# A four-layer conditioned sequence model on one core: which TensorE tilings stand next to each other in attention, MLP and experts

## Chip, core and metric

The kernel runs on one core of a Trainium2 chip. The metric is the device time of one execution in microseconds (us); less is better. The core has five engines that run side by side and wait for each other by semaphores: TensorE (PE, its weight loads are shown apart as PEld), VectorE (DVE), ScalarE (ACT), GpSimd (POOL) and SyncE (SP, which here issues DMAs).

## The reference, cut to what matters

The input is `x` of 4 sequences x 512 tokens x 288 channels in fp32 and a condition of 4 x 288. Four layers follow each other:

```python
x = x + (z @ expm(A(cond)) - z) @ U.T            # L0: z = x @ U, U from a QR of P
# L1 and L2: transformer blocks, modulated by cond; 16 heads of 18 channels
h = layernorm(x) * (1 + scale) + shift
q, k, v = split(h @ W_qkv + b_qkv)               # L2 also normalizes q and k per head
x = x + gate * (softmax(q @ k.T * 18**-0.5) @ v) @ W_proj
x = x + gate2 * gelu(modulate(layernorm(x)) @ w1 + b1) @ w2      # 288 -> 1152 -> 288
# L3: the same attention, then 4 experts, each token through its best 2
moe = sum_e cw[:, e] * (gelu(xn @ w1[e] + b1[e]) @ w2[e] + b2[e])
out = x + gate2 * moe
```

## The kernel before, in words

**Tilings.** TensorE can be used as one array of 128 rows x 128 columns or as smaller arrays side by side. A matmul's operands choose it: a contraction over 32 rows uses a 32x128 tiling (four such matmuls can run at once, on four row groups), an output of 32 partitions uses a 128x32 tiling (four at once, on four column groups). Every product of this kernel is in fp32, and the trace shows each matmul as two passes (a transpose as one).

**Channels.** The 288 channels are held as two slices of 128 (`KW = 2`) and a tail of 32, and the tail is repeated on three strips of 32 partitions (`strip(i)`). A product over channels is thus two dense matmuls (128x128 tiling) and one tail matmul (32x128 tiling), and the tails of up to three products can run side by side on three row groups.

**Blocks.** One attention block `n` (0 to 11) is one layer and one sequence; blocks 0 to 3 are layer L1, 4 to 7 L2, 8 to 11 L3. `attend(n, ...)` walks through 4 groups `G` of 4 heads, each in 8 steps `s`, so 32 steps a block. In each step

- `maxima` computes scores of two heads, 10 steps ahead (`p_s`, two matmuls of 32x128 tiling), and VectorE reduces them to row maxima (TENSOR_REDUCE `store<-p_s`);
- `weigh` computes the transposed scores of two other heads (`p_st`, two matmuls of 32x128 tiling, on the other two row groups, so beside `p_s`), and ScalarE takes the exponential (`e<-p_st`);
- in step `s = 6`, `take_maxima(G + 1)` transposes the maxima of the next group (`p_m`), and VectorE subtracts them from that group's queries (`store<-store,p_m`); `weigh` of the next group reads those queries from its step 0 on;
- in even steps `give_values` multiplies one key tile `c` (two steps' exponentials) with the values (`sum_values`, `p_av`, four matmuls of 128x32 tiling side by side); after the fourth key tile the sums are copied out (`o`);
- then other work fills TensorE: the generators in `fill`, each of which yields a cost after each piece. `left` grows by `total / 32` a step, 0.5 more in odd and 0.5 less in even steps, and pieces are taken while it is positive. The pieces are the next block's layernorm transposes (`p_t`) and projections (`project`: `p_qk`, `p_v`, in L2 also `p_var`), the last block's output projection (`finish`: `p_o`), and in blocks 10 and 11 the routing of tokens to experts (`route`, `place`). `norms` brings one piece of VectorE's layernorm work a step.

`project` goes through its products in pairs: the dense matmuls of both, then the two tails in one piece, then their evictions by ScalarE or VectorE. `p_s` and `p_st` share one PSUM ring of two buffers (`pbig`), so that each waits until the last one of its kind has been read. `pmm` is a PSUM ring of three buffers, used by nearly everything else; `pacc` is one buffer, for `p_av`.

**MLP.** After each of the blocks 1 to 8 the MLP of block `n - 1` runs alone (`mlp`, `hidden`, `mlp_out`): three groups of three hidden slices, each 12 dense passes (`p_h`), then the three tails side by side, then three Gelus; after the first group `between()` gives one key tile of values. Then `p_y`.

**Experts.** At the end 19 tiles of 256 tokens go through the experts (`tile_pieces`): again three groups of three slices (`p_he`: dense, tails, Gelus on ScalarE to `hide`), with a `yield` after each; then the transposes of the next tile (`p_te`, `p_tf`) and the second product (`p_ye`, 36 passes). At each yield a piece of the remaining routing (`others`) runs, six a tile, in tiles 0 to 3. POOL gathers a tile's weights and tokens and scatters its sums by indirect DMA.

**Order.** From the first column of L0 on, TensorE, ScalarE and VectorE keep the order in which the program text issues their instructions (`keep_in_program_order`), so the loops above are the order on the engines, and each engine runs its own list from the front.

Of the kernel before, what the change touches and what calls it, by code (L numbers as in the profile page):

```python
# [9 lines left out]
F32 = mybir.dt.float32  # L10
# [7 lines left out]
NT = 4  # L18
# [5 lines left out]
NG = 4  # L24
# [23 lines left out]
def cond_seq_kernel(ctx: ExitStack, tc: tile.TileContext, a: dict, out: bass.AP):  # L48
# [230 lines left out]
    md = mods.tile([128, C], F32, name="md")  # L279
# [17 lines left out]
    def modulations(ns):  # L297

        for n in ns:
# [4 lines left out]
            gr = mods.tile([B, C], F32, tag="gr", name=f"gr{n}")  # L304
# [11 lines left out]
            if half and l < 2:  # L316
                br = mods.tile([B, C], F32, tag="br", name=f"br{l}")
# [3 lines left out]
            if n == 5:  # L321
                sr = mods.tile([B, C], F32, tag="br", name="sr")
# [38 lines left out]
    with tc.tile_pool(name="l0", bufs=1) as l0, tc.tile_pool(name="l0w", bufs=2) as l0w, \  # L361
# [7 lines left out]
        At = mods.tile([D, C], F32, name="At")  # L369
# [327 lines left out]
    def hidden(pool, tag, bufs, l, b, h, w1, b1, func, between=lambda: None):  # L697

        gs = []
        for f0 in range(0, NF, 3):  # L700
            p = pbig(f"p_h{l}_{b}_{f0}")
            p = [p[:, 0, :], p[:, 1, :], pmm(f"p_h{l}_{b}_{f0 + 2}")]
            cols = [slice((f0 + i) * 128, (f0 + i + 1) * 128) for i in range(3)]
            for i in range(3):
                for k in range(KW):
                    matmul(p[i], w1[:, k, cols[i]], h[:, k, :], start=(k == 0), stop=False)
            for i in range(3):
                matmul(p[i], w1[strip(i), KW, cols[i]], h[strip(i), KW, :], start=False, stop=True)
# [6 lines left out]
            if f0 == 0:  # L715
                between()
        return gs
# [293 lines left out]
    with tc.tile_pool(name="attn", bufs=2) as at:  # L1011
# [15 lines left out]
        def project(n, norm):  # L1027

            l, b = divmod(n, B)
# [6 lines left out]
            def qk_job(m):  # L1036
# [4 lines left out]
                def evict():  # L1041
# [4 lines left out]
                    else:  # L1046
                        tmp = at.tile([128, 2, T], F32, tag="e", name=f"tmp{n}_{m}", bufs=6)
                        sq, rs = tmp[0:w, 0, :], tmp[0:w, 1, :]
# [24 lines left out]
            for i in range(0, len(jobs), 2):  # L1073
# [7 lines left out]
                for e in later:  # L1081
                    yield from e
                for q, (p, operands, evict) in enumerate(pair):
# [106 lines left out]
        def attend(n, fill, total, norms):  # L1190

            left = 0.0
            for step in range(8 * NG):
# [8 lines left out]
                if s == 8 - 2 and G + 1 < NG * NB:  # L1202
                    take_maxima(G + 1)
                if s % 2 == 0:
                    give_values()
                left += total / (8 * NG) + (0.5 if s % 2 else -0.5)
                next(norms, None)
                while left > 0:
                    cost = next(fill, "end")
                    if cost == "end":  # L1210
                        break
                    left -= cost or 0.0
# [7 lines left out]
        def give_values():  # L1220

            if not ready:
                return
            G, c = ready.pop()
# [289 lines left out]
```

## Time and profile before

| | |
|---|---|
| median of 3 runs | 2094.88 us (2086.53 to 2099.71) |
| the profiled execution | 2086.44 us |
| its span, first to last instruction | 2084.7 us |
| busy: PE / DVE / ACT / POOL | 91% / 45% / 37% / 12% |
| mean granted TensorE clock | 0.957 |
| attention blocks 0 to 11, with the MLPs between | 213.7 to 1647.5 us |
| experts | 1655.8 us to the end |
| scores' maxima on VectorE (384) | 470.4 us, 1225 ns each |
| exponentials on ScalarE (384) | 393.1 us, 1024 ns each |

A row of the profile names line, engine and operation, what is written and read (`out<-in`, buffer numbers left out), the shape, how many, and after a bar the busy time and mean duration and the idle time of the engine just before, with what ended it. In the timeline a row is a start, a time from first start to last end, and a merged group of like instructions; `[0.32 <-DVE store L60]` is idle time before it and what ended it. The page's busy time is an average over stages: a busy TensorE is not the same as a TensorE that sets the pace.

### The profile page before, as it was taken

To read this page: it belongs to the slowest core of one execution; us is meant where nothing else is said; L and a number is where in the kernel's file an instruction comes from. 1 tells how busy PE (TensorE), PEld (TensorE's weight loads), DVE (VectorE), ACT (ScalarE), POOL (GpSimd) and SP (SyncE) were. 2 spreads that over 40 slices of the span, in tenths; PEclk is the share of its full clock that TensorE was granted. 3 is DMA by queue.
4 is the path that set the end of the run, shared out by engine and by line. 5 is a ranking of instruction groups with operands and counts; after the bars stand their busy time and mean duration, and the time that the engine had idled before them with its cause. 6 is when DMAs were issued, how large, how long until landed. Compare 5 with 4: busy or idle time off the path is not lost. (4 is left out here: it accounts for less than half of the span.)

```text
span 2084.7 us, 26249 instructions
## 1 busy us (share of the span) xinstructions
PE 1901.0 (91%) x10269; PEld 927.7 (44%) x10269; DVE 928.8 (45%) x1953; ACT 781.3 (37%) x1169; POOL 252.2 (12%) x362
## 2 busy tenths in 40 slices
PE   6769879999999999899999999998987899999997
PEld 4544223343523434234234343333322367777775
DVE  6764646346164362562634526355576334111111
ACT  5122454434254343443444434444444322212111
POOL 1000010001010020010100000000000212332322
PEclk9578999999999999999999999999999989999999
DMA  3212152031131221511203112061221445766663
GB/s 97 71 40 62 37 153 81 17 96 29 40 73 26 72 58 42 135 42 54 75 22 85 33 54 80 23 137 30 82 50 61 172 147 175 238 187 219 203 202 95
DMA packets 89420, 187.23 MB, mean 90 GB/s; under 512 B 25454, under 2 KB 50457, under 8 KB 86803
## 3 DMA queue, kind: packets, MB, share of 16 engines
q1 hardware_dynamic: 77462, 103.39, 18.8%
q0 software_dynamic: 11248, 79.79, 11.8%
q10 hardware_dynamic: 584, 2.36, 0.4%
q8 instruction: 81, 1.33, 0.3%
q14 instruction: 45, 0.36, 0.1%
HBM read 152.49 MB, written 55.45 MB: 100 GB/s over the span
## 5 line engine op out<-in xcount | busy, mean ns | idle before, releaser
L60 DVE TENSOR_REDUCE store<-p_s 128x2 f32<-128x1024 f32 x384 | 470.4, 1225 | 370.3 <-PE p_st L60 324.0
L60 ACT ACTIVATE e<-p_st 128x1024 f32<-128x1024 f32 x384 | 393.1, 1024 | 643.9 <-PE p_st L60 639.6
L60 PE MATMUL p_s<-store 32*128 32x512 f32 x1536 | 445.4, 652 | 83.0 <-DVE store L60 81.7
L60 PE MATMUL p_st<-store 32*128 32x512 f32 x1536 | 444.2, 655 | 0.9 <-DVE store L60 0.9
L60 PEld LDWEIGHTS p_s<-store 32*128 32x128 f32 x1536 | 120.6, 186 | 315.9 <-DVE store L60 230.1
L60 PE MATMUL p_av<-e,store 128*32 128x512 f32 x1536 | 212.5, 626 | 2.0 <-ACT e L60 2.0
L60 PE MATMUL p_he<-hTe,store 128*128 128x256 f32 (+1 forms) x1026 | 200.1, 404 | 4.2 <-DVE hTe L60 4.2
L60 PE MATMUL p_ye<-store,hide 128*128 128x288 f32 x684 | 175.0, 415 | 7.2 <-ACT hide L60 7.2
L60 ACT ACTIVATE hide<-p_he,store 128x256 f32<-128x256 f32 x171 | 68.7, 472 | 281.7 <-PE p_he L60 281.7
L60 PEld LDWEIGHTS p_he<-hTe,store 128*128 128x128 f32 (+1 forms) x1026 | 147.7, 191 | 53.0 <-issue 30.5
L695 POOL TENSOR_TENSOR x<-x,gated 128x288 f32<-128x288 f32 x80 | 64.0, 800 | 837.0 <-DVE gated L60 837.0
L60 PE MATMUL p_qk<-hT,wqk 128*126 128x512 f32 (+1 forms) x360 | 162.3, 619 | 0.3 <-DVE store L60 0.3
L60 PE MATMUL p_h<-hT,w 128*128 128x512 f32 (+1 forms) x432 | 156.7, 618 | 5.2 <-DVE store L60 5.2
L60 PEld LDWEIGHTS p_ye<-store,hide 128*128 128x128 f32 x684 | 130.3, 193 | 46.9 <-ACT hide L60 11.0
L60 DVE TENSOR_TENSOR gated<-p_y,gate 128x288 f32<-128x288 f32 x32 | 14.7, 458 | 286.2 <-PE p_y L60 286.2
L60 PE MATMUL p_y<-w,hid 128*128 128x288 f32 x576 | 141.8, 407 | 0.0
L60 PEld LDWEIGHTS p_y<-w,hid 128*128 128x128 f32 x576 | 108.8, 190 | 35.5 <-issue 6.1
L60 PEld LDWEIGHTS p_st<-store 32*128 32x128 f32 x1536 | 118.0, 186 | 9.2 <-issue 6.2
L60 PEld LDWEIGHTS p_h<-hT,w 128*128 128x128 f32 (+1 forms) x432 | 60.7, 189 | 99.7 <-issue 83.6
L60 PE MATMUL p_o<-wp,oc 126*128 126x288 f32 (+1 forms) x288 | 94.6, 450 | 1.3 <-DVE oc L60 1.3
L60 DVE COPY hTe<-p_te 128x512 f32<-128x512 f32 x19 | 13.1, 690 | 172.9 <-PE p_tf L60 127.8
L60 PEld LDWEIGHTS p_qk<-hT,wqk 128*126 128x126 f32 (+1 forms) x360 | 46.9, 177 | 95.9 <-issue 94.3
(248 smaller groups left out, 1723.1 us busy)
## 6 DMA issues: line engine op xcount, KB each, us to landing
store<-qd SPq DMA_DIRECT2D x96, 144.0 KB
qd<-stage SPq DMA_DIRECT2D x48, 252.0 KB
od<-o SPq DMA_DIRECT2D x192, 36.0 KB
rd<-rd SPq DMA_DIRECT2D x12, 576.0 KB
oc<-od SPq DMA_DIRECT2D x24, 252.0 KB
rb<-rd SPq DMA_DIRECT2D x24, 252.0 KB
etab<-in_L_cond_w_dram SPq DMA_DIRECT2D x4, 1296.0 KB
etab<-in_L_cond_w_dram SPq DMA_DIRECT2D x8, 576.0 KB
```

The lines of the kernel that those rows point to most:

```text
L60: ins = f(*args, **kw)
L695: nc.gpsimd.tensor_add(x[b][:, j, :], x[b][:, j, :], t)
```

## The change

- **Values.** `give_values` gives all key tiles that are ready, oldest first, and `attend` calls it at steps 0 and 4 alone: two key tiles (8 matmuls of 128x32 tiling) in one run instead of one in each even step. These two steps take no fill piece; the other six take pieces, `left` growing by `total / 24` in each.
- **Projections' tails.** `project` yields `"strips"` ahead of a pair's tails. `attend` then stops taking pieces, and takes the tails first thing after the next step's scores.
- **Maxima.** `take_maxima` moves from `s = 6` to `s = 7`, behind that step's tails and `norms` piece and ahead of its fill pieces.
- **MLP.** The tails of the second group of three slices run at once after those of the first, as the first matmuls of their sums, and its dense passes follow later; `between()` now gives two key tiles.
- **Experts.** All nine tails of a tile run in one go: six slices' dense passes first (two slices to a PSUM bank), then nine tails, then six Gelus are issued, then the last three slices' dense passes and their Gelus. There are still six yields in a tile: after two slices, after four, after all nine, and then as before.
- **Buffers.** Small tiles (`md`, `gr`, `br`, `At`) become parts of one tile `spare`, and L2's squares and reciprocal deviations in `project` lie in it too, so that they no longer take buffers of the ring `e`. In block 2 `give_values` is called once more after the steps.

```diff
--- before.py
+++ after.py
@@ -276,7 +276,9 @@
-    md = mods.tile([128, C], F32, name="md")
+
+    spare = mods.tile([128, 4 * C], F32, name="spare")
+    md = spare[:, 0:C]
...
-            gr = mods.tile([B, C], F32, tag="gr", name=f"gr{n}")
+            gr = spare[0:B, C:2 * C]
...
-                br = mods.tile([B, C], F32, tag="br", name=f"br{l}")
+                br = spare[0:B, 2 * C:3 * C]
...
-                sr = mods.tile([B, C], F32, tag="br", name="sr")
+                sr = spare[0:B, 2 * C:3 * C]
...
-        At = mods.tile([D, C], F32, name="At")
+        At = spare[0:D, 3 * C:]
...
@@ -696,16 +698,32 @@
 
     def hidden(pool, tag, bufs, l, b, h, w1, b1, func, between=lambda: None):
 
+
         gs = []
+
+        def banks(f0):
+            p = pbig(f"p_h{l}_{b}_{f0}")
+            return [p[:, 0, :], p[:, 1, :], pmm(f"p_h{l}_{b}_{f0 + 2}")]
+
+        def cols(f):
+            return slice(f * 128, (f + 1) * 128)
+
+        def tails(p, f0, first):
+            for i in range(3):
+                matmul(p[i], w1[strip(i), KW, cols(f0 + i)], h[strip(i), KW, :], start=first, stop=not first)
+
         for f0 in range(0, NF, 3):
-            p = pbig(f"p_h{l}_{b}_{f0}")
-            p = [p[:, 0, :], p[:, 1, :], pmm(f"p_h{l}_{b}_{f0 + 2}")]
-            cols = [slice((f0 + i) * 128, (f0 + i + 1) * 128) for i in range(3)]
+            if f0 != 3:
+                p = banks(f0)
             for i in range(3):
                 for k in range(KW):
-                    matmul(p[i], w1[:, k, cols[i]], h[:, k, :], start=(k == 0), stop=False)
-            for i in range(3):
-                matmul(p[i], w1[strip(i), KW, cols[i]], h[strip(i), KW, :], start=False, stop=True)
+                    matmul(p[i], w1[:, k, cols(f0 + i)], h[:, k, :], start=(k == 0 and f0 != 3),
+                           stop=(k == KW - 1 and f0 == 3))
+            if f0 != 3:
+                tails(p, f0, False)
+            if f0 == 0:
+                ahead = banks(3)
+                tails(ahead, 3, True)
             for i in range(3):
                 f = f0 + i
                 if f % 2 == 0:
@@ -714,6 +732,7 @@
                 gs.append(t[:, f % 2, :])
             if f0 == 0:
                 between()
+                p = ahead
         return gs
 
     def mlp_out(l, b, j, gs, w2):
@@ -1026,6 +1045,7 @@
 
         def project(n, norm):
 
+
             l, b = divmod(n, B)
             wqk, wv = WA[l][:2]
             h = hT[0]
@@ -1044,8 +1064,7 @@
                     if l != 1:
                         scalar.activation(t, p[0:w], AF.Identity, bias=bias, scale=scol[0:w, m:m + 1])
                     else:
-                        tmp = at.tile([128, 2, T], F32, tag="e", name=f"tmp{n}_{m}", bufs=6)
-                        sq, rs = tmp[0:w, 0, :], tmp[0:w, 1, :]
+                        sq = rs = spare[0:w, m % 2 * T:(m % 2 + 1) * T]
                         scalar.activation(sq, p[0:w], AF.Square, bias=bias)
                         vector.tensor_scalar(t, p[0:w], bias, None, ALU.add)
                         yield 0.0
@@ -1080,6 +1099,7 @@
                     pair.append((p, operands, evict))
                 for e in later:
                     yield from e
+                yield "strips"
                 for q, (p, operands, evict) in enumerate(pair):
                     matmul(p, *operands(KW, strip(q)), start=False, stop=True)
 
@@ -1189,7 +1209,7 @@
 
         def attend(n, fill, total, norms):
 
-            left = 0.0
+            left, strips = 0.0, False
             for step in range(8 * NG):
                 g, s = divmod(step, 8)
                 G = NG * n + g
@@ -1199,17 +1219,22 @@
                         next(fill)
                     maxima(ahead, mstep)
                 E.append(weigh(G, s))
-                if s == 8 - 2 and G + 1 < NG * NB:
-                    take_maxima(G + 1)
-                if s % 2 == 0:
+                if strips:
+                    left -= next(fill)
+                    strips = False
+                next(norms, None)
+                if s % 4 == 0 and ready:
                     give_values()
-                left += total / (8 * NG) + (0.5 if s % 2 else -0.5)
-                next(norms, None)
-                while left > 0:
-                    cost = next(fill, "end")
-                    if cost == "end":
-                        break
-                    left -= cost or 0.0
+                else:
+                    left += total / (6 * NG)
+                    if s == 8 - 1 and G + 1 < NG * NB:
+                        take_maxima(G + 1)
+                    while left > 0:
+                        cost = next(fill, "end")
+                        strips = cost == "strips"
+                        if cost == "end" or strips:
+                            break
+                        left -= cost or 0.0
                 if s % 2:
                     ready.append((G, s // 2))
             for _ in fill:
@@ -1219,14 +1244,14 @@
 
         def give_values():
 
-            if not ready:
-                return
-            G, c = ready.pop()
-            if c == 0:
-                PO[0] = pacc(f"p_av{G}")
-            sum_values(G, PO[0], c, E[:2])
-            del E[:2]
-            if c == NT - 1:
+            while ready:
+                G, c = ready.pop(0)
+                if c == 0:
+                    PO[0] = pacc(f"p_av{G}")
+                sum_values(G, PO[0], c, E[:2])
+                del E[:2]
+                if c < NT - 1:
+                    continue
                 t = at.tile([128, T], F32, tag="o", name=f"o{G}", bufs=3)
                 scalar.copy(t, PO[0])
                 n, g = divmod(G, NG)
@@ -1296,7 +1321,8 @@
             if t == 8:
                 take_maxima(0)
             next(rest, None)
-            next(new)
+            if next(new) == "strips":
+                next(new)
             if t == 5:
                 projection_bias(0)
         for n in range(NB):
@@ -1352,6 +1378,8 @@
             if 2 <= n < 2 + 2 * NE:
                 fill_table(n - 2)
             attend(n, itertools.chain(*fill), total, first_ready(side))
+            if n == 2:
+                give_values()
             if n == 2 or n == B + 2:
                 projection_bias(l + 1)
                 head_biases(l + 1)
@@ -1422,19 +1450,45 @@
             w1, w2, b1, b2 = expert_tile(store[t % 2])
             h = HT.pop(t)
             g = pool2.tile([128, NF, TS], F32, tag="hid", name=f"hide{t}")
-            for f0 in range(0, NF, 3):
-                p = pbig(f"p_he{t}_{f0}")
-                p = [p[:, 0, :TS], p[:, 1, :TS], pmm(f"p_he{t}_{f0 + 2}")[:, :TS]]
-                cols = [slice((f0 + i) * 128, (f0 + i + 1) * 128) for i in range(3)]
-                for i in range(3):
-                    for k in range(KW):
-                        matmul(p[i], w1[:, k, cols[i]], h[:, k, :], start=(k == 0), stop=False)
-                for i in range(3):
-                    matmul(p[i], w1[strip(i), KW, cols[i]], h[strip(i), KW, :], start=False, stop=True)
-                for i in range(3):
-                    f = f0 + i
-                    scalar.activation(g[:, f], p[i], AF.Gelu_apprx_tanh, bias=b1[:, f:f + 1])
-                yield
+
+
+
+            def dense(f, first, last):
+                for k in range(KW):
+                    matmul(p[f], w1[:, k, f * 128:(f + 1) * 128], h[:, k, :], start=(first and k == 0),
+                           stop=(last and k == KW - 1))
+
+            def tails(fs, first):
+                for f in fs:
+                    matmul(p[f], w1[strip(f % 3), KW, f * 128:(f + 1) * 128], h[strip(f % 3), KW, :],
+                           start=first, stop=3 <= f < 6)
+
+            def gelus(fs):
+                for f in fs:
+                    scalar.activation(g[:, f], p[f], AF.Gelu_apprx_tanh, bias=b1[:, f:f + 1])
+
+            p = {}
+            for f0 in (0, 6):
+                q = pbig(f"p_he{t}_{f0}")
+                if f0 == 0:
+                    for n in range(2):
+                        for f in (3 * n, 3 * n + 1):
+                            p[f] = q[:, f % 3, n * TS:(n + 1) * TS]
+                            dense(f, n == 0, False)
+                        yield
+                    q = pmm(f"p_he{t}_2")
+                    for f in (2, 5):
+                        p[f] = q[:, f // 3 * TS:(f // 3 + 1) * TS]
+                        dense(f, f == 2, False)
+                    tails(range(6), False)
+                else:
+                    p[6], p[7], p[8] = q[:, 0, :TS], q[:, 1, :TS], pmm(f"p_he{t}_8")[:, :TS]
+                    tails(range(6, NF), True)
+                    gelus(range(6))
+                    for f in range(6, NF):
+                        dense(f, False, True)
+                    gelus(range(6, NF))
+            yield
             if t + 1 < TILES:
                 tokens_T(t + 1)
                 if t + 2 < TILES and t + 2 != EARLY:
```

## The prediction

> **What bounds the kernel now.** I read the page first, then the groups, the waits, and the timeline of one step. The page makes it TensorE, and the groups name its largest stops.
>
> ```profile
> PE 1901.0 (91%) x10269; PEld 927.7 (44%) x10269; DVE 928.8 (45%) x1953; ACT 781.3 (37%) x1169; POOL 252.2 (12%) x362
> ...
> L60 DVE TENSOR_REDUCE store<-p_s 128x2 f32<-128x1024 f32 x384 | 470.4, 1225 | 370.3 <-PE p_st L60 324.0
> ...
> L60 PE MATMUL p_s<-store 32*128 32x512 f32 x1536 | 445.4, 652 | 83.0 <-DVE store L60 81.7
> ```
>
> VectorE's maxima take 1225 ns each, and TensorE stood 81.7 us before scores, waiting for VectorE. The timeline of block 8 shows how:
>
> ```profile
> 1250.89 0.70 PE L60 MATMUL p_s<-store 32*128 32x512 f32 x2
> ...
> 1251.96 1.07 PE L60 MATMUL p_av<-e,store 128*32 128x512 f32 x8
> 1252.06 1.23 DVE L60 TENSOR_REDUCE store<-p_s 128x2 f32<-128x1024 f32 x1 [1.27 <-PE p_st L60]
> ...
> 1253.34 0.70 PE L60 MATMUL p_s<-store 32*128 32x512 f32 x2 [0.32 <-DVE store L60]
> ```
>
> Scores take 1.07 us (1250.89 to 1251.96); their maxima are done 1.33 later; the next scores start 2.45 after the last. So a step lasts at least **2.46 us**, or as long as TensorE's own work in it if that is more. Of 372 steps (31 in each block, the last one runs into the MLP) 110 last 2.44 to 2.48.
>
> **What a change of tiling costs.** Start-to-start times give it. Four dense passes of 512 columns between scores take 1.92 (708.70 to 710.62); the first MLP group after 1073.37 takes 6.41 to the values at 1079.78, for 12 dense passes and 2 slots of tails. 4a + b = 1.92 and 14a + 2b = 6.41 give a = 0.43 a pass and b = 0.20 a run, whatever its length. A run of one key tile's values takes 0.99 (1079.78 to 1080.77), so b = 0.14 there; its second pass starts 0.45 after the first (1.07 for the group less 0.62, the mean of one), so two key tiles in one run take 3 x 0.45 + 0.54 = 1.90 where two runs take 1.99. Other passes: 0.24 at 288 columns, 0.22 at 256, 0.11 for a transpose, b = 0.09 for a run of them.
>
> The built order has 1237 changes of tiling before and 956 after. Pricing each run so, TensorE's own work falls by 36 us in attention, rises by 1.5 in the MLPs (moved values) and falls by 13.6 in the experts: **48 us** in all.
>
> [...]
>
> **Attention steps.** For each of the 372 steps I added TensorE's work from its scores to the next scores in both built orders and took 2.46 where that is less. In block 8 before: 80.0 us of work, 13 steps below the floor and short of it by 7.1, sum 87.2; the trace has 87.2 (1240.0 to 1327.2). The first eight of block 8, in us of TensorE's work: 1.60 (scores 0.96 + 4 transposes), 3.21, 2.07 (scores 1.07 + one key tile 0.99), 2.98 (scores + four dense passes 1.92), 2.07, 3.09, 2.49, 2.98: four of eight are short. Over all blocks: 956 of work, 1045 with the floor, so 89 of waiting against 81.7 seen. The measured sum is 1100: 55 us of other waits (data of DMAs, layernorms, routing), which I leave as they are.
> After, block 8 begins 2.59, 2.13, 2.98, 2.13, 2.98, 0.96, 3.74, 2.46: work 76.3, 14 steps below, short by 10.0, sum 86.3. A step with two key tiles has 1.07 + 1.90 = 2.97, above the floor, and steps stopped at "strips" have as little as 0.96. All blocks: work 913, with the floor 1048. So 43 us of work go, and waiting for VectorE grows from 89 to 135: **+3**. (The 43 count only the 372 steps; the step that runs into an MLP takes 7 back.)
>
> **Maxima one step later.** Before, the subtraction had a whole step to itself; after, the next step's `p_st` waits for it. The row of its parts, at s = 6:
>
> ```profile
> 1257.38 0.66 PE L60 MATMUL p_m<-ident,store 128*128 128x128 f32 x4
> 1257.50 1.23 DVE L60 TENSOR_REDUCE store<-p_s 128x2 f32<-128x1024 f32 x1 [1.30 <-PE p_s L60]
> ...
> 1258.64 0.68 DVE L60 TENSOR_TENSOR store<-store,p_m 128x512 f32<-128x512 f32 x1
> ```
>
> The queries are ready 1258.64 + 0.68 - 1257.38 = 1.94 after the scores' end, 2.0 with the semaphore, so that step takes at least 1.07 + 2.0 = 3.07, plus what now stands between on VectorE: the `norms` piece and evictions. In the built order that is 0 to 1.2 (0.65 for four `rstd` operations, 0.63 for BATCH_NORM_STATS2 and AGGREGATE, 0.42 for `xn`). In block 8 the three boundaries hold 2.46, 3.26 and 1.60 of work and 0.65, 0.63 and 0.16 of such operations, so 1.26 + 0.44 + 0.77 = 2.5. All 12 blocks: **+24** (39 boundaries; those before an MLP have its time). Behind the waiting `p_st` stands all of TensorE; the scores `p_s` ahead of it run. The following step has two key tiles, above the floor, so nothing comes back. In the four L2 projections the `p_var` after `p_m` needs the buffer that the subtraction frees, 1.0 late: **+4**.
>
> **ScalarE.** At the start of a block three layernorm transposes now stand in one gap, so four evictions `hT` of 0.73 (three took 2.20 at 1244.61) come between two exponentials: 0.1 + 1.02 + 4 x 0.73 + 1.02 = 5.1 after the first scores, where the `p_st` that needs that buffer would come at 3.9 to 4.5. Before, an exponential stood between. 1.2 in four blocks and 0.65 in four, near 0 in the others: **+8**. The evictions ahead of the MLP's layernorm delay too, but the step after is below its floor and absorbs it.
> `p_var` pairs part, each alone in its gap; the wait of the second for PSUM, 0.78 in each of four blocks, goes: **-3**.
>
> **MLP.** One tail run of 0.4 less, `p_m` (0.53) and one key tile more: 39.0 to 39.7, eight times, +5.6; but `p_h` waited 0.87 for the maxima at each start, and `p_m` fills 0.53 of it: **+1.4**.
>
> **Experts.** A tile changes tiling 2 times instead of 6: 0.72 less, x 19 = -13.6. In the trace TensorE also waits for the last Gelu:
>
> ```profile
> 1821.00 0.44 PE L60 MATMUL p_te<-ident,xg 128*128 128x128 f32 x2
> 1821.12 1.20 ACT L60 ACTIVATE hide<-p_he,store 128x256 f32<-128x256 f32 x3 [2.22 <-PE p_he L60]
> ...
> 1822.37 5.85 PE L60 MATMUL p_ye<-store,hide 128*128 128x288 f32 x23 [0.49 <-ACT hide L60]
> ```
>
> After, six Gelus (2.4) run beside the last dense passes (2.7); the ninth ends 3.25 after the tails, the transposes 3.35. The 0.65 goes, in some 14 tiles: -9. Against it, two of six yields come after 1.8 us of work instead of 3.4, so routing steps in tiles 0 to 3 wait longer (one stood 4.0 us for VectorE already): +4. A tile takes 20.37 us now and 19.0 then; POOL's chain (weights' gather, two scatters, two token gathers) has 17 to 19 in it by its rows of the timeline, so it just fits. **-18.6**.
>
> **Nothing:** `spare` (the old tiles were single too), and moved evictions' DMAs: the block's last query and key tails stand in step 14 or 15 in both orders, so SP issues their stores and the loads of queries and keys when it did, 7 or more steps before the first scores that read them; `o` and its five DMAs stay at step 0 of the next group; POOL's list keeps its order. If the loads came a step late, 2.5 us in up to 11 blocks: part of the other waits below.
>
> **Sum.** 3 + 24 + 4 + 8 - 3 + 1.4 - 18.6 = **+18.8 us**: the profiled 2086.4 becomes 2105. The median shown lies 8.5 above that execution, so I forecast **2114**, 0.9% slower.
>
> **Unknown costs, both sides.** The experts' wait: -10 to 0, I take the trace's 0.65. Routing: 0 to +10. The subtraction: at 0 operations between, the boundaries give +12; at the built order's, +24, which I take; up to +30 if `rstd` waits for ScalarE. Other waits (55 us seen): -10 to +15, taken 0.
>
> **Rivals.**
> 1. TensorE sets the pace everywhere and the saving shows: -48 - 9 = -57, so 2038, or, with half of this, -28, so 2067. For it: 91% busy, 262 steps above 2.46. Against: saved time lands in steps already short. 0.15.
> 2. The experts give nothing, as POOL's chain of 19 us stretches when its transfers are pressed: +18.8 + 18.6 = +37, 2132. For it: one tile's gather took 14 us to land. Against: weights land 4 to 8 us before use. 0.10.
> 3. New waits chain: pairs of projections hold two of three `pmm` buffers a step longer, so that `p_m`, `p_t` and `p_var` wait behind their evictions: 0.5 at nine pairs in 11 blocks, +50, so +69 or 2164 at worst, about 2140 if half. Decides once evictions come more than a step late. 0.12.
> 4. The change doesn't part the runs as it says: excluded, the order shows 956.
>
> The forecast's own case, 0.63: 2095 to 2130. A measurement of this kernel tells about 1% (21 us) from no change; the case lies across that line. Range 2067 to 2146: from half of rival 1 to rival 3's middle. Faster 0.15, same 0.39, slower 0.46.
>
> **What would show it.** Right: TensorE's waits before `p_s` for VectorE's maxima rise from 82 to over 120 us; a new row, `p_st` waiting for `store<-store,p_m`, of 15 to 30 us; an expert tile at 19.0. Wrong: blocks shorter than before by 3 us or more each (rival 1); tiles at 20.4 (rival 2); waits of `p_m` or `p_qk` for `stage` (rival 3).

## The result, and the profile after

The changed kernel takes **2144.2 us** (median of 4 runs, 2140.0 to 2147.5) against 2094.3 before (4 runs, 2086.5 to 2099.7): a ratio of 1.025, 95% interval 1.021 to 1.029, **slower**. The forecast was 2114. The profiled executions took 2086.4 before and 2140.0 after; everything below compares these two unless it says otherwise.

From the page of the changed kernel, first busy times, then the clock by slices, then three groups (busy time, mean ns | idle time before them and what ended most of it):

```profile
PE 1916.5 (90%) x10269; PEld 959.8 (45%) x10269; DVE 929.7 (43%) x1953; ACT 785.3 (37%) x1169; POOL 252.6 (12%) x362
...
PEclk9579979999899999999999999999888889999999
...
L60 DVE TENSOR_REDUCE store<-p_s 128x2 f32<-128x1024 f32 x384 | 470.4, 1225 | 451.6 <-PE p_st L60 398.5
...
L60 PE MATMUL p_s<-store 32*128 32x512 f32 x1536 | 454.3, 668 | 108.3 <-DVE store L60 105.0
L60 PE MATMUL p_st<-store 32*128 32x512 f32 x1536 | 453.4, 668 | 3.2 <-DVE store L60 2.0
```

TensorE has as many matmuls as before (10269), fewer changes of tiling, and yet 15 us more busy time. Its wait for the maxima rose from 81.7 to 105.0. The mean of a score matmul rose from 652 to 668 ns. Nothing in the diff makes a matmul longer, so this row asks for the clock, and the mean granted clock fell from 0.957 to 0.940. The same row of slices before:

```profile
PEclk9578999999999999999999999999999989999999
```

By stages, the windows of after for blocks 0, 8 and 10 (31 steps each; length, busy time of five engines, granted clock, DMA share, GB/s), and the same blocks before:

```profile
213.70:309.90 96.20, 75.83 (x482) 21.88 (x482) 45.96 (x54) 41.88 (x63) 2.70 (x7) 0.89 0.35 92
1274.80:1364.70 89.90, 80.86 (x475) 28.80 (x474) 53.12 (x77) 44.70 (x54) 3.97 (x5) 1.00 0.24 72
1499.00:1619.30 120.30, 103.61 (x552) 38.52 (x548) 62.22 (x110) 44.56 (x55) 6.17 (x8) 0.83 0.21 55
```

```profile
213.70:298.10 84.40, 71.12 (x490) 20.75 (x490) 44.88 (x53) 41.68 (x63) 1.68 (x5) 0.96 0.30 80
1240.00:1327.20 87.20, 80.67 (x492) 28.30 (x492) 53.93 (x78) 44.60 (x54) 3.97 (x5) 1.00 0.24 74
1456.80:1554.70 97.90, 89.53 (x555) 32.91 (x556) 62.05 (x110) 44.63 (x55) 5.99 (x8) 0.97 0.25 68
```

Block 8 ran at full clock in both, and there the terms of the forecast add up to what was measured: 86.3 for the steps, 2.5 for the subtraction and 1.2 for ScalarE make 90.0, and it took 89.9. Blocks 0 and 10, where the clock fell from 0.96 to 0.89 and from 0.97 to 0.83, lost 11.8 and 22.4 us. So the first theory after the result was: **the terms of the forecast hold, and what is missing is the clock**. The trace records every change of the granted clock; in before and after it is either full or half (1.0 or 0.5). From the first block on its stretches at half last 3.41, 6.83 or 10.24 us, but for the one that reaches over the program's end, and in each of the two traces all of them start on one grid of 3.41 us (to 3 ns). After 213.7 us (the first block's start) TensorE stood at half clock for 93 us before and 170 us after. The rival: the half clock is only a symptom of waits, and it is ordinary waits (VectorE's order, PSUM buffers, the stop ahead of tails) that cost the 35 us.

### The profile page after: what moved, and what is told of

It is laid out like the page before. It is cut to its first block, busy times and chain, and to the rows that moved or that the text cites. A ratio compares the mean times of both kernels' runs of the same rounds, so it can differ in the third digit from the quotient of the medians.

```text
span 2138.3 us, 26244 instructions
## 1 busy us (share of the span) xinstructions
PE 1916.5 (90%) x10269; PEld 959.8 (45%) x10269; DVE 929.7 (43%) x1953; ACT 785.3 (37%) x1169; POOL 252.6 (12%) x362
## 3 DMA queue, kind: packets, MB, share of 16 engines
q8 instruction: 81, 1.33, 0.3%
## 5 line engine op out<-in xcount | busy, mean ns | idle before, releaser
L60 PE MATMUL p_s<-store 32*128 32x512 f32 x1536 | 454.3, 668 | 108.3 <-DVE store L60 105.0
L60 PE MATMUL p_st<-store 32*128 32x512 f32 x1536 | 453.4, 668 | 3.2 <-DVE store L60 2.0
L60 PE MATMUL p_av<-e,store 128*32 128x512 f32 x1536 | 205.4, 656 | 0.1
L60 PE MATMUL p_he<-hTe,store 128*128 128x256 f32 (+1 forms) x1026 | 192.0, 394 | 5.8 <-DVE hTe L60 4.3
L60 PEld LDWEIGHTS p_he<-hTe,store 128*128 128x128 f32 (+1 forms) x1026 | 153.1, 193 | 41.6 <-issue 17.1
L60 PEld LDWEIGHTS p_av<-e,store 128*32 128x32 f32 x1536 | 42.6, 116 | 147.5 <-issue 145.8
```

The lines of the kernel that those rows point to most:

```text
L60: ins = f(*args, **kw)
```

## What an us at half clock costs

No experiment had to be made for this: the clock differs between runs of one program. Over 105 runs of 12 kernels (those below included), the span rises by **0.45 us for each us at half clock** (time at half clock from each run's mean clock, differences within one kernel on one chip only; standard error 0.013). At half clock matmuls take about twice as long (in the last section's lines a step's scores hold TensorE for 2.00 us instead of 1.06, start to start), so by my estimate about 0.5 is the most that it can be (0.94 of 2.00 in these lines).

The traces show it in single stretches too. The kernels before and e1_experts (below) have the same instructions until the experts. Blocks 5 and 6, of before and then of e1_experts (same columns as above):

```profile
832.90:932.10 99.20, 88.84 (x499) 30.25 (x500) 60.66 (x88) 50.43 (x64) 11.73 (x10) 0.97 0.38 93
972.00:1069.50 97.50, 91.43 (x501) 30.68 (x502) 60.58 (x88) 50.50 (x64) 11.73 (x10) 0.95 0.22 66
```

```profile
835.10:939.10 104.00, 94.07 (x499) 31.42 (x500) 60.77 (x88) 50.51 (x64) 11.73 (x10) 0.92 0.37 89
979.00:1072.00 93.00, 86.62 (x499) 29.38 (x500) 60.47 (x88) 50.43 (x64) 11.73 (x10) 1.00 0.23 69
```

The same block 5 is 4.8 us longer with 0.92 instead of 0.97, the same block 6 is 4.5 shorter with 1.00 instead of 0.95, with VectorE's and ScalarE's busy times unchanged.

And in a single step. The kernels after and e7_nogive (below) are the same there. TensorE's timeline of after ahead of and in the fall of the clock, then that of e7_nogive:

```profile
240.23 0.70 PE L60 MATMUL p_s<-store 32*128 32x512 f32 x2 [0.63 <-DVE store L60]
...
242.68 0.70 PE L60 MATMUL p_s<-store 32*128 32x512 f32 x2 [0.63 <-DVE store L60]
...
245.13 0.87 PE L60 MATMUL p_s<-store 32*128 32x512 f32 x2 [1.31 <-DVE store L60]
```

```profile
246.64 1.16 PE L60 MATMUL p_v<-wv,hT 32*128 32x288 f32 x2
247.73 2.50 PE L60 MATMUL p_av<-e,store 128*32 128x512 f32 x16
250.16 0.70 PE L60 MATMUL p_s<-store 32*128 32x512 f32 x2
```

```profile
245.32 0.70 PE L60 MATMUL p_s<-store 32*128 32x512 f32 x2 [1.31 <-DVE store L60]
...
246.28 0.64 PE L60 MATMUL p_v<-wv,hT 32*128 32x288 f32 x2
246.85 1.92 PE L60 MATMUL p_av<-e,store 128*32 128x512 f32 x16
```

In after the clock fell at 245.5: the tails of `p_v` took 1.16 instead of 0.64, the values 2.50 instead of 1.92, and the step 5.03 us instead of 3.39. The longest idle stretch of TensorE in the 8 us ahead of the fall was 1.31 us. The steps before were alike to 0.01 us in both runs; what differed is where they lay on the 3.4 us grid (the next step's scores start at 250.16 and 248.71).

## The experiments

Half clock is the time at half clock after 213.7 us in the kernel's own trace, so of one execution. By the mean clocks of all runs, over the whole program, after has 267 us, e2_max6 270 and e4_nostop 271; e9_strips has 178 where the kernel before has 184 on the same chip, so its 63 is that of its fastest run. All ratios are to the kernel before on the same chip; its medians there, 2084.7 to 2088.9, are lower than the 2094.3 of the first row, so compare ratios and not medians.

| kernel | median us | ratio (95%) | half clock us |
|---|---|---|---|
| before | 2094.3 | 1 | 93 |
| after | 2144.2 | 1.025 (1.021 to 1.029) | 170 |
| e1_experts | 2077.6 | 0.995 (0.991 to 0.999) | 85 |
| e2_max6 | 2137.8 | 1.023 (1.018 to 1.029) | 189 |
| e3_warm | 2140.5 | 1.026 (1.022 to 1.030) | 105 |
| e4_nostop | 2144.2 | 1.027 (1.022 to 1.032) | 182 |
| e5_warm2 | 2136.1 | 1.022 (1.017 to 1.027) | 126 |
| e6_exp_warm | 2067.3 | 0.989 (0.985 to 0.993) | 78 |
| e7_nogive | 2144.0 | 1.028 (1.022 to 1.033) | 175 |
| e8_pairs | 2139.1 | 1.022 (1.015 to 1.029) | 185 |
| e9_strips | 2106.9 | 1.010 (1.006 to 1.013) | 63 |
| e10_max7 | 2105.9 | 1.007 (1.003 to 1.010) | 96 |

### e1_experts: the experts' part alone

`tile_pieces` of the changed kernel in the kernel before, nothing else.

> The kernel before with the experts' part of the change alone (dense passes and tails of nine expert columns in two runs of tails). My sum gave this part -18.6 us. The trace of after has tiles of 19.03 instead of 20.37 from the fifth on, but tiles 2 and 3 took 28.8 and 27.4 instead of 26.8 and 22.1. If the part is as it looks there: 14 to 15 tiles x 1.34 = -19 to -20, less 6 to 7 lost in the first tiles: -12 to -14 us against before. If the first tiles lost time only through the clock left low by the blocks ahead of them, -19 or better. If the experts give nothing (rival 2 of the prediction), within 3 us of before.

-0.5%, some 10 us (3 to 18); in the traces the experts' stage, from its first matmul to the end, goes from 428.9 to 413.8. The part does what the forecast said, a little less of it. A tile takes 19.03 us in it from the fifth on, as in after, whose lines stand further down.

### e2_max6: the subtraction back in the seventh step

```diff
                 E.append(weigh(G, s))
+                if s == 8 - 2 and G + 1 < NG * NB:
+                    take_maxima(G + 1)
...
                     left += total / (6 * NG)
-                    if s == 8 - 1 and G + 1 < NG * NB:
-                        take_maxima(G + 1)
```

> The changed kernel with the subtraction of the maxima put back to the seventh step of a group, right after the weights' step, where the kernel before has it. My sum priced the later place at +24 us. If that term is right and the clock plays no part in it: 20 to 28 us faster than after. If the larger part of the 50 us is the clock that falls to half in steps with scores alone, and the later subtraction costs only what block 8 showed (2.5 us) in some blocks: 5 to 20 faster. If VectorE's order is not what costs (rival): within 5 us of after.

A miss for the +24: it stands within the noise of after, as the rival had it. Block 8 (no half clock in either) shows where it went. The eighth steps became 1.33, 0.77 and 0.95 us shorter, the seventh 1.13, 1.13 and 0.12 longer. TensorE's timeline of e2_max6:

```profile
1281.92 1.12 PE L60 MATMUL p_qk<-hT,wqk 32*126 32x512 f32 x4
1283.31 1.98 PE L60 MATMUL p_qk<-hT,wqk 128*126 128x512 f32 x4 [0.27 <-DVE store L60]
```

`p_m` takes one of three `pmm` buffers until VectorE has subtracted. In the changed order a pair of projections stands behind it in the seventh step, and the second pair waits for that buffer. The wait belongs to the order as a whole, not to the place of the subtraction alone.

### e3_warm and e5_warm2: keep TensorE busy in light steps

```diff
+                if ran[0] < 0.6 and step < 8 * NG - 1:
+                    p = pmm(f"p_warm{G}_{s}")
+                    for i in range(4):
+                        matmul(p[:, i * 128:(i + 1) * 128], ident, ident, start=True, stop=True)
```

`ran` counts TensorE's time of a step's other work. e5_warm2 has `ran[0] < 0.2 and s != 7 and step < 8 * NG - 2` instead.

> The changed kernel, with four products of the identity with itself (128x128, 0.87 us of TensorE's time, result unused) added to every attention step whose work beside scores and values comes to less than 0.6 us; 70 steps have it. It only adds work. Theory of the clock: these are the stretches in which TensorE is busy less than half of a window of 3.4 us and the clock falls to half; the time at half clock after the first 214 us, 170 us now, falls below 110, and the kernel is 15 to 35 us FASTER than after. Theory of ordinary waits (VectorE, PSUM buffers, routing): the work lies in waits or costs up to 9 us by my sum of steps, so 0 to 15 us slower than after.

> The changed kernel with the four idle products of the identity again (0.87 us of TensorE, result unused), but only in steps that have scores and nothing else, never in a group's last step (there the products waited 1.0 to 1.5 us for the PSUM buffer that the subtraction frees) and not in a block's last two. e3_warm brought the time at half clock from 170 to 105 us after 214 us and yet gained nothing; step by step it gained where the clock had been half (-2.6, -2.6, -2.5 us in single steps) and lost 1.0 to 1.5 at each group's end. Theory of the clock: without those losses the gain shows, half clock near 110 us and 12 to 25 us faster than after (2120 on the scale where after is 2137 to 2140). Theory of ordinary waits: the dummies' own cost was small and the clock costs nothing: within 5 us of after.

Both brought the half clock down (170 to 105 and 126), and neither gained what that is worth (29 and 20 us at 0.45). In the total the theory of the clock missed both times: e3_warm came out within 5 us of after, inside what the theory of ordinary waits had forecast, and e5_warm2 some 7 us faster by the ratios, where the two theories had 12 to 25 and at most 5. The single steps tell the two theories apart. Where a light step had been followed by a half-clock step, the gain is there. TensorE's timeline of after, block 11, and the same step in e3_warm:

```profile
1658.28 3.64 PE L60 MATMUL p_av<-e,store 128*32 128x512 f32 x16
```

```profile
1657.38 1.16 PE L65 MATMUL p_warm<-ident 128*128 128x128 f32 x8
1658.76 0.70 PE L65 MATMUL p_s<-store 32*128 32x512 f32 x2 [0.23 <-DVE store L65]
...
1659.84 1.92 PE L65 MATMUL p_av<-e,store 128*32 128x512 f32 x16
```

That step fell from 5.59 to 2.96 us, one in block 0 from 5.57 to 2.93, one in block 10 from 5.59 to 3.05: more work in the step ahead, less time. Against it, in e3_warm the products of a group's last step waited for the buffer that the subtraction frees (1.0 longer in blocks 0, 2, 7, 8 and 10), and in three places the clock fell where it had not fallen in after (one step each: +2.4 in block 5, +2.1 in block 8, +4.0 in block 10). In e5_warm2 the savings met other waits: block 0's last steps wait for the next layer's weights, which VectorE could first read at 307.0 to 307.7 us in after, e3_warm and e5_warm2 alike (one step went from 3.76 to 7.95 us in e5_warm2), `stage` for its store (+1.9 in block 5), and in blocks 10 and 11 the clock fell in other places (+2.5, +1.8, +2.1). So the clock costs time, but buying it back with work of no use in this schedule cost about as much. These single steps do not add up to the whole of the missing 29 and 20 us.

### e4_nostop, e9_strips: the stop ahead of the tails, taken out and put in alone

e4_nostop, on the changed kernel:

```diff
-                        strips = cost == "strips"
-                        if cost == "end" or strips:
+                        if cost == "strips":
+                            cost = next(fill)
+                        if cost == "end":
                             break
```

> The changed kernel without the stop ahead of a projection's tails: they follow their dense passes within the same step, at any time. By my sum of steps (TensorE's work, at least 2.46 a step): 1048 becomes 1033, so -15 us, and 41 instead of 60 steps have scores alone. Theory of the clock: fewer such steps also leave the clock up; the time at half clock falls from 170 to under 130 us, so in all 20 to 35 us faster than after. Theory that the two-key runs or the maxima's place cost the time: the 15 of my sum at most, or nothing.

> Of the change only the stop ahead of a projection's tails, on the kernel before: the tails then stand directly behind the next step's scores. By my sum of steps 1073 against 1045 before, so +28 us, because pairs of projections and the stops leave 40 instead of 16 steps with scores alone while others grow. With the clock (half clock 120 to 140 us instead of 93, at 0.44 us each as the runs of one kernel show) +12 to +20 more: 30 to 45 us slower than before. If the stop is harmless, as e4_nostop would have it (taking it out of the changed kernel gave nothing): within 10 us of before.

e4_nostop gave nothing. e9_strips cost about 20 us, and at no more half clock than before has (63 in its trace, 178 against 184 over the runs): the sum of steps (+28) was about right, the clock's part of the expectation was wrong. So here steps with scores alone did not bring the clock down by themselves, where values stand in every second step. That clears the stop of the fall of the clock (not of its own 20 us in the order of before), and it sharpens the theory: what counts would be a whole 3.4 us of light steps.

### e7_nogive: the values ahead of the third block's biases

```diff
-            if n == 2:
-                give_values()
```

> The changed kernel without the values given ahead of the third block's biases (they stand in its MLP, as in every other block). That MLP with what precedes it took 53.3 us in after against 45.5 before, 12.8 of them at half clock. If the early values pull TensorE's work out of the stretch in which it waits for POOL's gains: 48 to 50 us there, half clock 3 to 7, and 3 to 6 us faster in all. If the place of the values is of no account: the same 53.

A miss of the 3 to 6 us: the wait for POOL's gains there went (2.0 us), but the clock stayed low for 16.6 instead of 12.8 us, and the stretch took 52.7 instead of 53.3, as if the place of the values were of no account.

### e8_pairs: the values' part alone

The changed kernel with the stops, the place of the subtraction, the MLPs' tails and the experts set back to before: left are the values of two key tiles in one run, every fourth step (and between an MLP's groups), the other work in the remaining steps, and the buffers.

> Of the change only the values of two key tiles in one run, and what they need (buffers, pace of the other work): no stops ahead of tails, the subtraction at the seventh step, MLPs and experts as before. By my sum of steps 1030 against 1045 before, so -15 us; ScalarE's evictions in one gap +8, the subtraction with a pair of projections behind it +10 to 12 (block 8 of e2_max6), so near +4 without the clock. Theory of the clock: 30 steps have scores alone (16 before, 41 in e4_nostop), half clock 130 to 150 us against 93: another +20, so 20 to 30 us slower than before. If the stops and the MLPs are to blame for the clock: within 8 us of before.

**+2.2%, nearly the whole loss, with 185 us at half clock**: more than expected in both. By the mean clocks of all runs it has 77 us more at half clock than before; at 0.45 these are 35 of the 47 us by which the runs' mean is longer, and some 12 are left for the +4 of the sum. Block 8 took 86.8 us in it, a little less than the 87.2 before; so at full clock the pairs do no harm. The windows of e8_pairs for blocks 8, 10 and 11:

```profile
1264.10:1350.90 86.80, 79.73 (x483) 29.16 (x482) 53.48 (x78) 44.88 (x54) 3.96 (x5) 1.00 0.26 74
1478.70:1591.20 112.50, 97.12 (x558) 37.01 (x558) 62.40 (x110) 44.78 (x55) 6.17 (x8) 0.86 0.21 59
1593.60:1700.90 107.30, 89.18 (x452) 30.55 (x452) 48.94 (x102) 36.15 (x41) 9.29 (x11) 0.73 0.21 72
```

### e10_max7: the late subtraction alone, in the order of before

```diff
-                if s == 8 - 2 and G + 1 < NG * NB:
-                    take_maxima(G + 1)
...
                 next(norms, None)
+                if s == 8 - 1 and G + 1 < NG * NB:
+                    take_maxima(G + 1)
```

> The kernel before with one edit: the subtraction of the maxima in the eighth step of a group, after the norms, where the changed kernel has it. The prediction gave this place +24 us in the changed order. In the order of before the eighth step has 3.0 us of TensorE's work or more at most groups' ends, against the 3.07 that the maxima's chain takes plus 0 to 0.65 of VectorE's other operations: +0.3 to +0.7 at 39 ends, so +8 to +15 us, with the clock as before. If the place alone costs what the prediction said: +24. If the seventh step gives back what the eighth loses, as block 8 of e2_max6 did: within 5 us of before.

+0.67%, some 14 us: the sum of steps was right to its range. With e2_max6 this says how the +24 has to be read: in the order of before the late place costs some 14; in the changed order, taking it back gained nothing clear of the noise, since the seventh step then grew.

### e6_exp_warm: experts' part and idle products on the kernel before

e1_experts with the lines of e5_warm2.

> The kernel before with the experts' part of the change, and the same idle products in its steps that have scores alone (15 or so). e1_experts had 85 us at half clock after 214 us, of which 51 lie in the blocks' attention. Theory of the clock: 20 to 30 us less at half clock, at 0.5 us each: 8 to 15 us faster than e1_experts, so 0.985 to 0.990 of before. Ordinary waits: the same as e1_experts, 0.995.

0.989, the fastest of all, 1.1% below before, and steady: six runs from 2062.8 to 2070.0, where e1_experts has 2062.3 to 2088.3. By the ratios it is 0.6% below e1_experts, but the two were not run on the same chip and their intervals overlap, so that the idle products gain anything is likely and not shown. Half clock fell by 7 us only in the profiled pair; over the runs' mean clocks the medians are 167 and 191 us, so -24 at 0.45 = -11 us, in line with the expectation.

## Why the prediction fell short, by its own steps

**The step that failed** is the sentence "The measured sum is 1100: 55 us of other waits (data of DMAs, layernorms, routing), which I leave as they are", and its bound "-10 to +15, taken 0". In the trace of before 61 us of the 372 steps ran at half clock; at 0.45 that is 28 of the 55. That half was no wait for data but TensorE's clock, and it moved with what the change moves: how TensorE's work is spread. With the change, half clock grew by 77 us, 34.7 us at 0.45, where the bound allowed 15 for all other waits together. The page of before showed the clock (0.957). The forecast had no term for it; its steps are priced at one clock.

| part | forecast us | measured us | us more at half clock | these at 0.45, us | rest |
|---|---|---|---|---|---|
| attention steps | +36 | +45.3 | 48.3 | 21.7 | +23.6 |
| blocks' last steps and MLPs | +1.4 | +18.4 | 23.1 | 10.4 | +8.0 |
| experts | -18.6 | -10.2 | 5.8 | 2.6 | -12.8 |
| sum | +18.8 | +53.5 | 77.2 | 34.7 | **+18.8** |

The column at 0.45 is the one before it times the 0.45 of the runs, so the split is an estimate. Without the clock the rest is the forecast; that the sums agree to a decimal is luck, since attention came out 12 us better and the other two 12 worse.

- **Floors of the steps.** Block 8 held (89.9), block 10 too, once the clock is taken off: by the same sum for that block, +3.8 for floors and +3.8 for the subtraction, 7.6; measured +22.4, of which 34 us more at half clock make 15.3, leaving 7.1. The announced sign was missed: TensorE's waits before `p_s` for the maxima rose to 105, not over 120.
- **Maxima one step later, ScalarE's evictions.** Right in size; the sign was announced in the wrong place. The `p_st` row shows 3.2 us of waits, not 15 to 30. The profile of after at block 8's first group end, all engines:

```profile
1296.62 0.65 PE L60 MATMUL p_m<-ident,store 128*128 128x128 f32 x4
...
1298.07 1.13 PE L60 MATMUL p_s<-store 32*128 32x512 f32 x4
...
1298.53 0.68 DVE L60 TENSOR_TENSOR store<-store,p_m 128x512 f32<-128x512 f32 x1
...
1299.36 1.13 PE L60 MATMUL p_st<-store 32*128 32x512 f32 x4 [0.17 <-DVE store L60]
```

`p_st` starts 1.29 us after its `p_s`, where 0.01 is usual: it stands until the subtraction's end (1299.21). But `p_s`, ahead of it, counts as busy until 1299.20, so only 0.17 is booked as idle. Summed over all steps, `p_st` lagged its `p_s` by 7.8 us before and by 35.6 after: +27.8 for the forecast's 24 + 8. Block 8's three ends alone show 1.29, 0.39 and 1.02 (2.5 were worked out as 1.26 + 0.44 + 0.77), and 1.14 behind ScalarE (1.2). In e2_max6, with the subtraction back in the seventh step, the lag is 15.1, and in e10_max7, with the late place alone, 26.7: some 19 to 21 us of it belong to the late place. In e2_max6 the longer seventh steps took their place.
- **MLPs.** Those at full clock took 40.1 to 40.8 instead of 39.9, +0.2 to +0.9 where +0.17 was worked out for each. The terms that the prediction names (one tail run less, `p_m`, a key tile more) add up to +1.0 a block, not to its +0.7, and so to near +4 instead of +1.4. The third block's took 53.3 instead of 45.5: 9.4 us more at half clock (4.2) and 2.0 of waiting for POOL's gains, a wait that I did not see; e7_nogive, without the early values, does not have it. The other 1.6 have no cause shown.
- **Experts.** A tile takes 19.03 us; 19.0 was forecast. From the timelines of after, TensorE and ScalarE, from one tile's first matmul to the next's (1878.56 to 1897.59):

```profile
1878.56 9.63 PE L60 MATMUL p_he<-hTe,store 128*128 128x256 f32 x54
...
1888.76 9.00 PE L60 MATMUL p_ye<-store,hide 128*128 128x288 f32 x36
1897.59 4.70 PE L60 MATMUL p_he<-hTe,store 128*128 128x256 f32 x21
```

```profile
1885.06 3.64 ACT L60 ACTIVATE hide<-p_he,store 128x256 f32<-128x256 f32 x9 [14.79 <-PE p_he L60]
```

The nine Gelus end at 1888.70, before `p_ye` begins, and `p_ye` has no wait; POOL's chain fits. The total gain was put too high: ten tiles take 19.03, but the last four 19.1 to 20.1, and the third and fourth took 28.8 and 27.4 instead of 26.8 and 22.1, +7.3 where I had put +4 for the routing steps. Of that, 6.8 us more at half clock in the fourth tile make 3.1 (in e1_experts, without any there, it takes 24.7); the rest is the 4.
- **Rivals.** 1 is out: blocks 2 and 8, at full clock in both kernels (block 2 but for 0.8 us), are 2.6 and 2.7 longer. 2 is out by the tile. 3 named waits of evictions for buffers; `stage` waits for its store 5.3 us in all, not 50. That 2144 lies close to rival 3's 2140, and just inside the upper end of the range, 2146, that was drawn for it, is luck: it got there by the clock and not by those waits.

## Why the pairs bring the clock down

For each window of the 3.4 us grid I worked out the share of time in which matmuls ran, from their columns and the duration of a pass at the clock of that window (the ends of matmuls are modelled in these traces, so the shares are estimates; worked out with 0.42 to 0.44 us for a pass of 512 columns, the counts shift and the picture stays). Over the twelve traces of this case (before, after and ten experiments), from the first block on:

| share of a window | full clock before it: windows, of them followed by half | half clock before it: windows, of them followed by full |
|---|---|---|
| below 0.3 | 125, 125 | 20, 0 |
| 0.3 to 0.4 | 85, 64 | 8, 0 |
| 0.4 to 0.5 | 200, 53 | 7, 0 |
| 0.5 to 0.6 | 372, 4 | 32, 0 |
| 0.6 to 0.8 | 1466, 2 | 78, 18 |
| 0.8 to 0.9 | 1993, 0 | 132, 76 |
| above 0.9 | 2007, 0 | 153, 142 |

So in these traces a window below 0.3 lost the clock (125 of 125), one of 0.3 to 0.4 mostly (64 of 85), one above 0.5 hardly ever (6 of 5838). To get it back took a window above 0.6 (below that, 0 of 67), and only above 0.9 did it come back nearly always (142 of 153). In the kernel before, values stand in every second step (4.9 us), so a window of 3.4 us nearly always holds part of a run of values. With values in every fourth step, 7.4 us hang on the other work alone; a step with scores alone is busy 0.96 of 2.46 us, 0.39. Such stretches come where the other work is thin (block 0, block 10 behind its projections, each block's end). After has 27 falls of 6.3 us on average, before 19 of 4.9; the falls last longer too, I think because the light steps that follow do not fill a window. What e8_pairs, e9_strips and e4_nostop (185, 63 and 182 us at half clock) show is that the values' part brings most of the fall and the stop does not. That it is the spacing of the values, rather than the uneven pace of the other work that comes with it, is argued and was not tried by itself.

In these traces the longest gap does not tell where the clock falls. In the attention of after TensorE was never idle for more than 2.62 us at a time, and yet it fell: the fall at 245.5 came after no idle stretch above 1.31 us, in a window with a share of 0.37. Nor is it one case: of the 175 falls in the attention of the twelve traces, 160 came with no idle stretch of 3 us in or at the window ahead. Here the fall goes with the share and not with the longest gap. The share, as worked out here, is not the whole rule either: the window of e7_nogive over the same steps has 0.36 and kept the clock.

## What to carry to other kernels

Ask of a change that evens out or gathers TensorE's work what it does to the busiest and the emptiest 3.4 us, not only to the sum: gathering work into fewer, longer runs here left windows in which TensorE was busy less than 0.4 of the time, and each us at half clock that followed cost 0.45 us. Price the time at half clock in the trace of before as a term of its own, or it hides among "other waits" and moves with the change. Fewer changes of tiling paid where TensorE had next to no idle time beside them (the experts: 1.34 us a tile, of which some 0.5 to 0.65 is the wait for the last Gelu that went), and where another engine set the step they only moved its wait (in attention TensorE stood 105.0 us before scores for the maxima, 81.7 before the change). The version to keep is the experts' part alone; with idle products in the steps that have nothing but scores it measured best (0.989).

## What the runs showed of the hardware that I had not expected

**The half clock stayed for 34.1 us, with TensorE never idle.** TensorE's timeline at block 11's end in e8_pairs, and of the same work in after:

```profile
1671.13 2.08 PE L60 MATMUL p_st<-store 32*128 32x512 f32 x4
1673.13 3.64 PE L60 MATMUL p_av<-e,store 128*32 128x512 f32 x16
1676.71 2.08 PE L60 MATMUL p_st<-store 32*128 32x512 f32 x4
1678.71 3.54 PE L60 MATMUL p_o<-wp,oc 126*128 126x288 f32 x6
1682.19 2.08 PE L60 MATMUL p_st<-store 32*128 32x512 f32 x4
```

```profile
1697.35 1.13 PE L60 MATMUL p_st<-store 32*128 32x512 f32 x4
1698.41 1.92 PE L60 MATMUL p_o<-wp,oc 126*128 126x288 f32 x6
1700.26 1.13 PE L60 MATMUL p_st<-store 32*128 32x512 f32 x4
```

The rows follow one another without a gap, and yet the clock stayed at half: 5.5 us a step instead of 2.9. By columns the windows there have shares of 0.80 to 0.92. The same instructions in after have 0.79 to 0.89 and kept the full clock. So between about 0.5 and 0.9 the full clock stayed (6 falls in 3831 windows), while the half clock often stayed too (with shares of 0.6 to 0.9 it came back after 94 of 210 windows), and a stretch of such work was fast or slow, I think by how it was entered: block 11 took 88.8 us in after and 107.3 in e8_pairs and e2_max6. Nine windows in a row with a share of 0.8 or more did not bring it back; the tenth, with a share of 0.97, did.

**The same instructions met either clock.** Two runs of the same instructions, alike to 0.01 us in the steps before, had half clock in one and not in the other (block 0, above). They lay differently on the 3.4 us grid, but the window that kept the clock has no larger share (0.36 against 0.37), so what decided between them is not shown. The spread of the runs of one kernel goes with the clock, 2074.5 to 2103.9 us for the kernel before over all its runs: the slower ones have the lower mean clock (0.949 at 2102.2 us of span, 0.962 at 2072.8).
